# Half of a weight matrix loaded during attention, a weight test handed from VectorE to GpSimd, and one wait of ScalarE put on another instruction

## The chip, the cores and the metric

The kernel runs on one core of a Trainium2 chip. It is one program on one core: TensorE (PE), VectorE (DVE), ScalarE (ACT) and GpSimd (POOL) each work through their own instructions in order, and DMAs are issued in order on queues that belong to an engine: the queue of SyncE (SP), of ScalarE and of GpSimd. The metric is the device time of one execution in microseconds (us), as the median of several runs. Lower is better.

## The reference

`x` is 4 batches of 1024 tokens with 256 channels, float32. There are 16 heads of 16 channels, and the hidden width of the feed-forward part is 1024. The weights of the feed-forward part are ternary (-1, 0 or 1) with a scale per output.

```
x = x + layernorm(attention(layernorm(x)))       # q, k, v, p: alpha * sign(W), softmax over 1024 keys
x = x + layernorm(ffn(layernorm(x)))

def ffn(x):
    h = silu(x @ w1.T * s1) * (x @ w2.T * s2)    # 256 -> 1024
    h = gelu(h @ h1.T * sh1)                     # 1024 -> 1024
    h = gelu(h @ h2.T * sh2)                     # 1024 -> 1024
    return h @ w3.T * s3                         # 1024 -> 256
```

## The kernel before, in words

Products run in TensorE's reduced-precision float format (`F32R`), with every activation split into a high and a low piece, so that two products give nearly full precision. The weights are taken as they are, in one piece. That is right only when their low bits are zero, as they are for ternary weights. So the kernel looks at every weight of the feed-forward part during attention: it collects their low bits in the tile `bits`, reduces them at the end to a flag (`any_bits`, `decide`), and branches on the flag before the feed-forward part to `mlp("", False, ...)` or to a slower form. With these inputs the fast form runs.

**Attention** is a loop over steps `s`, written out in the order of the program. A step handles 128 keys for a block of 512 queries and four heads; 8 steps make a block (`STEPS`), 16 steps a unit `u` of four heads (2 blocks), 64 steps a batch, and there are 256 steps. Each step has two halves. In a half step TensorE does six products of the second pass (`second_pass`, L690), four of the first pass (`first_pass`, L642) for a step that lies ten steps ahead, and the product of the weights with `v` for the step before (`attend`, L707). VectorE takes the row maximum of the first pass (`first_max`, L652) and ScalarE the exponential of the second pass (`second_exp`, L695), both out of PSUM. The exponentials go to tiles `e` from a pool of five buffers, two exponentials for each tile.

Everything else is a job in the dictionary `jobs`, which `place` puts behind a half step `(s, slot)`; `run_jobs` issues the jobs of a half step at its end, and so they stand on each engine's queue at that place. The jobs that matter here, for unit `u` that starts to be used by the first pass at `s = 16u - 10`:

- `group_jobs` (for even `u`): the q and k projections of the next two units, in four `part`s at `16u - 24, -22, -20, -18`, slot 1. Each is a product, a ScalarE copy out of PSUM (L500), and on GpSimd a cast and a subtraction (L506, L507) that write the high and low pieces to the tiles q0, q1, k0, k1. Each of the four tiles is 128 x 1024 in float32 and has one buffer.
- `spread(u)` at `16u - 16`, slot 0: 24 DMAs on SyncE's queue (L530) that copy rows of these pieces to the layout of the products, `qs` and `ks` with two buffers each. The first-pass products of a new unit wait for the first 12 in its first half step and for the last 12 in its second.
- `batch_jobs`: norms, transposes and `v` of the next batch; `project_jobs`: the output projection of the finished batch (z times `az_bc` plus `bz_bc` on GpSimd at L574 and L575), its moments, and `finish_tile` on GpSimd (L589, L592).
- `turn_y`, `divide`, `return_y`: the result of a block is transposed on VectorE (L727), divided on GpSimd (L733), transposed back on VectorE (L748) and sent by four DMAs on SyncE's queue (L751).
- `weight_jobs`: loads of `w1`, the first half of `h1` (`h1a_sb`) and `w2` on GpSimd's queue (L821); then 44 `gather` jobs, one for each 128 x 512 tile of the weights, that put its bits into `bits` (L835). The first 12 and the last 4 take tiles that stay; the 28 between take tiles that are only looked at (second half of `h1`, `h2`, `w3`), loaded into `wraw` with two buffers. `take(i)` gathers tile i and then issues the load of tile i + 2 on SyncE's queue (L840), which waits until the gather has read the buffer.

`tc.add_manual_dep(a, b)` makes instruction a wait for instruction b. A tile of a pool that comes round again makes its first writer wait for what last wrote and read that buffer; an instruction carries one wait, and what it has to wait for besides goes into a waiting instruction put ahead of it.

**The feed-forward part** (`mlp`) loads the second half of `h1` (`h1b_sb`, 2 MB in 2 DMAs), then `h2` (4 MB) and `w3` on GpSimd's queue (L1009) once GpSimd has finished its last work of attention. It then runs 8 blocks of 512 tokens: `gated` (w1 and w2), `hidden` with `h1`, `hidden` with `h2` (all products at L1063) and `down` (L1177).

Of the kernel before, what the change touches and what calls it, by code (L numbers as in the profile page):

```python
# [30 lines left out]
F32 = mybir.dt.float32  # L31
F32R = mybir.dt.float32r
I32 = mybir.dt.int32
AF = mybir.ActivationFunctionType
ALU = mybir.AluOpType
AX = mybir.AxisListType
# [3 lines left out]
P = 128  # L40
# [5 lines left out]
def sandwich_kernel(  # L46
# [23 lines left out]
    nc = tc.nc  # L70
# [35 lines left out]
    w1_sb = const.tile([P, KC, F], F32R, tag="w1", name="w1_sb")  # L106
    w2_sb = const.tile([P, KC, F], F32R, tag="w2", name="w2_sb")
    h1a_sb = const.tile([P, NF // 2, F], F32R, tag="h1a", name="h1a_sb")


    xnT_sb = const.tile([P, KC, T], F32R, tag="xnT", name="xnT_sb")
# [114 lines left out]
    def attention(signs):  # L226


        with ExitStack() as actx:
# [83 lines left out]
            nc.gpsimd.memset(negmax, 0.0)  # L313

            a2 = actx.enter_context(tc.tile_pool(name="a2", bufs=2))
            a3 = actx.enter_context(tc.tile_pool(name="a3", bufs=5))
            av = actx.enter_context(tc.tile_pool(name="av", bufs=1))

            def binarize(w, sgn, dst):
# [159 lines left out]
            def group_jobs(grp):  # L479

                b, c = divmod(grp, KC)

                def part(is_q, j, engine=nc.gpsimd):
                    tag = "q" if is_q else "k"
                    if j == 0:
                        pieces_of[grp, is_q] = [
                            ac.tile([P, T], F32R, tag=f"{tag}{i}", name=f"{tag}{i}_{grp}")
                            for i in range(2)
                        ]
                    t = bank(grp > 0)  # L490
# [14 lines left out]
                    hi, lo = (t[:, bass.ts(j, 512)] for t in pieces_of[grp, is_q])  # L505
                    engine.tensor_copy(hi, full)  # L506
                    engine.tensor_sub(lo, full, hi.bitcast(F32))  # L507

                if grp == 0:
                    return part  # L510
                return [lambda i=i, j=j: part(i, j) for i in (True, False) for j in range(NQ)]
# [179 lines left out]
                    [nmT_by[blk]] if n == 2 else [],  # L691
                )

            def second_exp(s, g, t):
                got([t], "ACT", nc.scalar.activation(  # L695
                    e_of[s][g // 2][:, g % 2, :], through[:, t, :], AF.Exp
                ))

            def attend(s, part):

# [51 lines left out]


            jobs = {}
            beside_pe = []

            def place(at, job, on_pe=False):
                jobs.setdefault(at, []).append(job)
                if on_pe:
                    beside_pe.append(at)  # L760

            first = -STEPS - LEAD
            for b in range(1, B):
                norms, turns, values = batch_jobs(b)
                at = b * NG * NQ * STEPS + first
                for i, job in enumerate(norms):
                    place((at - 32 + i // 2, i % 2), job)
                for i, job in enumerate(turns):
                    place((at - 18 + i // 2, i % 2), job, True)

                for i, job in enumerate(values):
                    place((at - first - STEPS + 3 + 2 * i, 0), job, True)
            for u in range(1, B * NG):
                at = u * NQ * STEPS + first
                if u % 2 == 0:
                    for job, when in zip(group_jobs(u // 2), (-14, -12, -10, -8)):
                        place((at + when, 1), job, True)
                place((at - 6, 0), lambda u=u: spread(u))
            for b in range(B):
                for half in range(2 if b < B - 1 else 1):  # L780
                    at = (((b + 1) * NG - 1) * NQ + half + 1) * STEPS + (6, 10)[half]
                    pieces, projects, measures, finishes = project_jobs(b, half)
                    for i, job in enumerate(pieces):
                        place((at - 2, i), job)
                    for i, job in enumerate(projects):
                        place((at + i, 1), job, True)
# [21 lines left out]


            raw_of = {}  # L810
            bits = ac.tile([P, 512], I32, tag="bits", name="bits")
            nc.gpsimd.memset(bits, 0)

            def weight_jobs():
# [17 lines left out]
                        ]  # L832

                def gather(w):
                    nc.vector.tensor_tensor(bits, bits, w.bitcast(I32), ALU.bitwise_or)  # L835

                def load(i):
                    if i < len(pass_by):
# [10 lines left out]

                def any_bits():  # L850

                    nc.vector.tensor_scalar(bits, bits, 0xFFF, None, ALU.bitwise_and)
                    nc.vector.tensor_reduce(some, bits, AX.X, ALU.max)
                    nc.vector.tensor_scalar(some, some, 0.0, None, ALU.is_gt)

# [18 lines left out]

            free = (B * NG - 2) * NQ * STEPS + first - 6
            place((free, 0), last)
            at = 44
            for job in gathers + last_gathers:
                if job is last_gathers[0]:
                    at = max(at, free + 6)  # L880
                at, slot = min((k for k in beside_pe if at + 3 <= k[0] <= at + 5), default=(at + 4, 1))
                place((at, slot), job)

            def run_jobs(s, slot):
                for job in jobs.pop((s, slot), ()):
# [21 lines left out]
            for s in range(first, total + 2):  # L907
# [4 lines left out]
                for half in range(2):  # L912


                    second_of, first_of = [], []
                    if second:
                        e_of[s].append(a3.tile([P, 2, 512], F32, tag="e", name=f"e_{s}_{half}"))
                    two, pair = take(2 * second, 2 * (a < total))
                    if second:
                        second_of = list(zip((2 * half, 2 * half + 1), two))  # L920
                    if a < total:

                        first_of = [
                            (2 * (1 - half) + t - min(pair), t, begin) for begin, t in enumerate(pair)
                        ]
                    for n in range(3):
                        for g, t in second_of[:1]:
                            second_pass(s, g, t, n)
                        for g, t, begin in first_of:
                            if 0 <= n - begin < 2:  # L930
                                first_pass(a, g, t, n - begin)
                        for g, t in second_of[1:]:
                            second_pass(s, g, t, n)
                    for g, t in second_of[:1]:
                        second_exp(s, g, t)
                    if a < total:
                        first_max(a, pair, 1 - half)
                    if 0 <= s - 1 < total:
                        attend(s - 1, half)
                    if s > 0 and (s % STEPS, half) == (0, 1):  # L940
                        fetch_y(s // STEPS - 1)
                    for g, t in second_of[1:]:
                        second_exp(s, g, t)
# [11 lines left out]
    def mlp(tag, low_too, wp):  # L955
        with ExitStack() as fctx:

            def pool(name, bufs, **space):
# [11 lines left out]

            blocks = B * T // 512
            per_batch = T // 512
            h1b_sb = fw.tile(
                [P, NF // 2, F], F32R, tag="h1b", name="h1b_sb" + tag
            )
            h2_sb = fw.tile([P, NF, F], F32R, tag="h2", name="h2_sb" + tag)
            w3_sb = fw.tile([P, NF, C], F32R, tag="w3", name="w3_sb" + tag)

            w1_w, w2_w, h1_w, h2_w, w3_w = (
                (w1_sb,), (w2_sb,), (h1a_sb, h1b_sb), (h2_sb,), (w3_sb,)  # L980
            )

            def rows(w, k):
# [16 lines left out]
                )  # L1000
                return raw[:, :n, :]

            for dst, wT, parts in (
                (h1b_sb, h1T[F // 2 : F, :], 2), (h2_sb, h2T, 4), (w3_sb, w3T, 1)
            ):
                n = dst.shape[1] // parts
                for i in range(parts):
                    ks = bass.ts(i, n)
# [320 lines left out]
```

## Time and profile before

| What | Value |
|---|---|
| median of 3 runs (lowest to highest) | 1643.37 us (1639.27 to 1645.26) |
| profiled execution, its own time | 1643.64 us |
| profiled execution, span of the instructions | 1641.8 us |
| busy share PE / DVE / ACT / POOL | 96% / 66% / 51% / 21% |
| attention, from its first to its last product | about 45 to 968 us |
| 44 gathers on DVE (L835) | 32.7 us busy |
| mean granted TensorE clock | 0.981 |

All times of the profile are of one execution. A group of instructions has a line, an engine and an operation; behind the bar stand its busy time and the mean of one in ns, and then the idle time of the engine just before it with what ended that idle time. The TensorE clock is the share of full speed that was granted.

### The profile page before, as it was taken

What the parts mean: (1) busy time and instruction counts of PE and PEld (TensorE: products, weight loads), DVE (VectorE), ACT (ScalarE), POOL (GpSimd) and SP (SyncE); (2) the same over time, 40 slices, a digit from 0 to 9 for tenths busy, and PEclk for the clock granted to TensorE, in tenths of its full rate; (3) what the DMA queues carried; (4) which work ended last, traced back from release to release, by engine and by line L of the source; (5) the groups of instructions that cost most, each with busy time, mean ns of one, the idle gap of its engine ahead of it and who ended that gap; (6) DMA issues with size and microseconds to landing.
All of it is one profiled execution on the core that took longest, in us unless ns stands there. A gap on an engine that the chain in (4) does not pass through costs nothing.

```text
span 1641.8 us, 31481 instructions
## 1 busy us (share of the span) xinstructions
PE 1574.0 (96%) x12964; PEld 1010.1 (62%) x12964; DVE 1079.7 (66%) x1497; ACT 844.2 (51%) x1481; POOL 347.7 (21%) x484
## 2 busy tenths in 40 slices
PE   4699999999999999999999998999999999999997
PEld 3344444544445444445544457888888888888886
DVE  4578878889887889787789633563636363535453
ACT  2067777776777676777776771132323232323231
POOL 1011320454011343104511042120202020202011
PEclk9689999999999999999999999999999999999999
DMA  1502242202331232132122005000000000000000
GB/s 56 105 2 46 63 90 47 43 19 71 69 64 42 49 69 52 38 66 43 24 53 47 5 7 179 1 13 1 13 1 13 1 14 0 14 0 14 1 14 16
DMA packets 35673, 60.10 MB, mean 37 GB/s; under 512 B 10176, under 2 KB 21696, under 8 KB 35520
## 3 DMA queue, kind: packets, MB, share of 16 engines
q1 hardware_dynamic: 29568, 44.35, 12.7%
q0 software_dynamic: 3760, 11.54, 2.2%
q10 hardware_dynamic: 2192, 2.10, 0.6%
q8 instruction: 104, 1.70, 0.4%
q14 instruction: 49, 0.40, 0.1%
HBM read 24.40 MB, written 4.19 MB: 17 GB/s over the span
## 4 chain that ended last, share of the span: by engine, by line
PE 83%; DVE 9%; DMA 2%; ACT 1%; POOL 1%; issue 1%; SPq 1%; ACTq 0%; DVEq 0%; POOLq 0%
PE g L1063 28%; PE through L690 18%; PE y L707 14%; PE p L1063 7%; PE through L642 6%; DVE nm L652 6%; PE fzp L1177 4%; PE through L493 2%; DMA qs<-q 1%; PE through L670 1%; PE through L560 1%; SPq L530 1%; PE through L451 1%; DMA ks<-k 1%; DVE bits L835 1%
## 5 line engine op out<-in xcount | busy, mean ns | idle before, releaser
L652 DVE TENSOR_REDUCE nm<-through 128x2 f32<-128x1024 f32 x512 | 619.6, 1217 | 144.6 <-PE through L690 107.2
L695 ACT ACTIVATE e<-through 128x512 f32<-128x512 f32 x1024 | 557.3, 596 | 216.4 <-PE through L690 178.7
L642 PE MATMUL through<-ks,qs 32*128 32x512 f32 x2048 | 473.8, 452 | 15.6 <-DMA ks<-k 10.9
L690 PE MATMUL through<-qs,ks 32*128 32x512 f32 x2048 | 397.8, 448 | 13.0 <-DVE nm L652 12.5
L707 PE MATMUL y<-e,v 128*32 128x256 f32 x4096 | 337.5, 393 | 0.0
L690 PEld LDWEIGHTS through<-qs,ks 32*128 32x128 f32 x2048 | 203.0, 184 | 213.1 <-issue 134.1
L642 PEld LDWEIGHTS through<-ks,qs 32*128 32x128 f32 x2048 | 240.3, 187 | 28.4 <-issue 12.1
L1063 PE MATMUL g<-g,h_sb 128*128 128x512 f32 x1024 | 235.8, 390 | 0.0
L690 PE MATMUL through<-nmT,ones_r 32*128 32x512 f32 x1024 | 219.9, 394 | 0.0
L1063 PEld LDWEIGHTS g<-g,h_sb 128*128 128x128 f32 x1024 | 191.7, 188 | 39.6
L707 PEld LDWEIGHTS y<-e,v 128*32 128x32 f32 x4096 | 83.8, 108 | 193.3 <-issue 174.4
L1106 ACT ACTIVATE g2f<-g,sh_sb 128x512 f32<-128x512 f32 x64 | 44.1, 688 | 200.5 <-PE g L1063 173.6
L1106 ACT ACTIVATE g1f<-g,sh_sb 128x512 f32<-128x512 f32 x64 | 44.0, 689 | 177.8 <-PE g L1063 174.9
L1063 PE MATMUL g<-h,h1b_sb 128*128 128x512 f32 x512 | 127.8, 392 | 4.6 <-DMA h1b_sb<-in_dram 4.6
L1063 PE MATMUL g<-h,h1a_sb 128*128 128x512 f32 x512 | 128.1, 393 | 0.0
L1033 DVE CAST g<-g2f 128x512 fp32r<-128x512 f32 x64 | 27.8, 434 | 142.0 <-ACT g2f L1106 142.0
L1063 PE MATMUL p<-xnT_sb,w_sb 128*128 128x512 f32 x512 | 118.0, 390 | 1.2 <-DVE hf L1139 1.2
L690 PEld LDWEIGHTS through<-nmT,ones_r 32*128 32x128 f32 x1024 | 108.9, 185 | 6.1
L1063 PEld LDWEIGHTS g<-h,h1b_sb 128*128 128x128 f32 x512 | 96.9, 190 | 25.1 <-issue 5.0
L1063 PEld LDWEIGHTS g<-h,h1a_sb 128*128 128x128 f32 x512 | 97.2, 190 | 20.5
L1063 PEld LDWEIGHTS p<-xnT_sb,w_sb 128*128 128x128 f32 x512 | 95.5, 188 | 21.6 <-DVE hf L1139 1.7
L146 POOL TENSOR_SCALAR ve_fz<-mvp_fz 128x4 f32<-128x4 f32 (+1 forms) x8 | 1.9, 233 | 470.8 <-DVE mvp_fz L158 470.8
(173 smaller groups left out, 1438.9 us busy)
## 6 DMA issues: line engine op xcount, KB each, us to landing
qs<-q SPq DMA_DIRECT2D x248, 64.0 KB, 2.4
ks<-k SPq DMA_DIRECT2D x124, 64.0 KB, 2.4
wraw<-in_dram SPq DMA_DIRECT2D x28, 256.0 KB, 2.7
h_sb<-in_dram POOLq DMA_DIRECT2D x4, 1024.0 KB, 11.5
yT<-yt SPq DMA_DIRECT2D x112, 32.0 KB, 1.9
out_dram<-x_sb SPq DMA_DIRECT2D x7, 512.0 KB, 2.8
x_sb<-in_dram SPq DMA_DIRECT2D x3, 1024.0 KB, 6.0
w_sb<-in_dram POOLq DMA_DIRECT2D x3, 1024.0 KB, 8.7
```

The lines of the kernel that those rows point to most:

```text
L451: put(t, nc.tensor.matmul(through[:, t, bass.ts(i, C)], xnT[j][:, k, bass.ts(2 * m + i, P)], w_in["v"][:, k, :], start=(k == 0 and j == 0) ...
L493: put(t, nc.tensor.matmul(through[:, t, :], w_in[tag][:, k, bass.ts(c, P)], xnT[i][:, k, bass.ts(j, 512)], start=(k == 0 and i == 0), stop ...
L530: queue.dma_start(dst[to, :].bitcast(F32), src[rows, :].bitcast(F32))
L642: put(t, nc.tensor.matmul(through[:, t, :], q_of[u][n][rows, bass.ts(qt, P)], k_of[u][rows, bass.ts(j, 512)], start=(n == 0), stop=(n == 1),))
L652: got(banks, "DVE", nc.vector.tensor_reduce(nm_of[blk][:, n4, j, 2 * pair : 2 * pair + 2], through[:, min(banks) : max(banks) + 1, :], AX. ...
L690: t, nc.tensor.matmul(through[:, t, :], lhs, rhs, start=(n == 0), stop=(n == 2)),
L695: got([t], "ACT", nc.scalar.activation(e_of[s][g // 2][:, g % 2, :], through[:, t, :], AF.Exp))
L707: nc.tensor.matmul(y_of[blk][32 * g : 32 * g + 32, cols], v_sb[n // 2][:, n % 2, :, :].rearrange("p h d -> p (h d)")[:, bass.ds((4 * g4 + ...
L1033: nc.vector.tensor_copy(hi, full)
L1063: nc.tensor.matmul(out[c], wk, src[j][:, k, :], start=(k == 0 and i == 0 and j == 0), stop=(k == n_k - 1 and i == len(ws) - 1 and j == 1),)
L1106: nc.scalar.activation(g, ps, AF.Gelu, scale=scale[:, c : c + 1])
L1177: nc.tensor.matmul(out_ps[i][:, :C], g2[j][:, k, bass.ts(i, P)], wk, start=(k == 0 and n == 0 and j == 0), stop=(k == NF - 1 and n == len( ...
```

## The change

- The four tiles q0, q1, k0, k1 become the four tiles `h1b0` to `h1b3` of the constant pool, each 128 x 1 x 1024. When the last spread has read them, four loads of 0.5 MB on GpSimd's queue at steps 226 to 229 fill them with the second half of `h1`. `mlp` loads only `h2` and `w3`.
- A `gather` is two GpSimd operations: a copy that turns the low 16 bits of each weight (every second half word) into floats, and an addition to `bits`, now float32. The mask with 0xFFF in `any_bits` goes; the rest of `any_bits` stays on VectorE.
- The gathers get other places. Before, each went 3 to 5 steps behind the last, beside a job with products where there was one. Now the first 40 go at steps 47, 51, ..., slot 1 (every step that is 3 or 7 modulo 8); the load of the first two `wraw` tiles takes one of these places. The last four gathers, `any_bits` and `decide` go at steps 214 to 219.
- The second exponential of each `e` tile gets a manual dependence on the second exponential four tiles before it, which is the one whose buffer the next tile takes. The wait of ScalarE for itself then stands on the second exponential of a tile, no longer on the first.

The order of the products, of ScalarE's instructions and of the DMAs other than those of `wraw` and `h1b` stays as it was; `decide`'s product comes earlier.

```diff
+    h1b_sb = [
+        const.tile([P, 1, F], F32R, tag=f"h1b{i}", name=f"h1b{i}_sb") for i in range(NF // 2)
+    ]
...
                         pieces_of[grp, is_q] = [
-                            ac.tile([P, T], F32R, tag=f"{tag}{i}", name=f"{tag}{i}_{grp}")
-                            for i in range(2)
+                            t[:, 0, :] for t in (h1b_sb[:2] if is_q else h1b_sb[2:])
                         ]
...
-            def second_exp(s, g, t):
-                got([t], "ACT", nc.scalar.activation(
+            def second_exp(s, g, t, last):
+                exp = got([t], "ACT", nc.scalar.activation(
                     e_of[s][g // 2][:, g % 2, :], through[:, t, :], AF.Exp
                 ))
+                if last:
+                    last_exps.append(exp)
+                    if len(last_exps) > E_TILES - 1:
+                        tc.add_manual_dep(
+                            exp, last_exps[-E_TILES].name, SYNC, reason="the next tile"
+                        )
...
-            bits = ac.tile([P, 512], I32, tag="bits", name="bits")
+            bits = ac.tile([P, 512], F32, tag="bits", name="bits")
...
                 def gather(w):
-                    nc.vector.tensor_tensor(bits, bits, w.bitcast(I32), ALU.bitwise_or)
+                    low = w.bitcast(U16).rearrange("p (c half) -> p c half", half=2)[:, :, 0]
+                    half = ac.tile([P, 512], F32, tag="half", name="half")
+                    nc.gpsimd.tensor_copy(half, low)
+                    nc.gpsimd.tensor_add(bits, bits, half)
...
                 def any_bits():
-                    nc.vector.tensor_scalar(bits, bits, 0xFFF, None, ALU.bitwise_and)
                     nc.vector.tensor_reduce(some, bits, AX.X, ALU.max)
...
+            for i, to in enumerate(h1b_sb):
+                place(
+                    (free + NQ * STEPS + 2 + i, 0), lambda to=to, i=i: nc.gpsimd.dma_start(
+                        to[:, 0, :], h1T.rearrange("(k p) o -> p k o", p=P)[:, NF // 2 + i, :]
+                    ),
+                )
             at = 44
             for job in gathers + last_gathers:
                 if job is last_gathers[0]:
                     at = max(at, free + 6)
-                at, slot = min((k for k in beside_pe if at + 3 <= k[0] <= at + 5), default=(at + 4, 1))
-                place((at, slot), job)
+                while at % STEPS not in (3, 7) and job not in last_gathers:
+                    at += 1
+                place((at, 1), job)
+                at += 1
...
-            h1b_sb = fw.tile(
-                [P, NF // 2, F], F32R, tag="h1b", name="h1b_sb" + tag
-            )
...
-            for dst, wT, parts in (
-                (h1b_sb, h1T[F // 2 : F, :], 2), (h2_sb, h2T, 4), (w3_sb, w3T, 1)
-            ):
+            for dst, wT, parts in ((h2_sb, h2T, 4), (w3_sb, w3T, 1)):
```

More of the change, by code (lines that the diff above doesn't have):

```diff
@@ L33 @@
 I32 = mybir.dt.int32
+U16 = mybir.dt.uint16
 AF = mybir.ActivationFunctionType
@@ L315, in attention @@
             a2 = actx.enter_context(tc.tile_pool(name="a2", bufs=2))
-            a3 = actx.enter_context(tc.tile_pool(name="a3", bufs=5))
+            E_TILES = 5
+            a3 = actx.enter_context(tc.tile_pool(name="a3", bufs=E_TILES))
             av = actx.enter_context(tc.tile_pool(name="av", bufs=1))
@@ L692, in second_pass @@
                 )
-            def second_exp(s, g, t):
-                got([t], "ACT", nc.scalar.activation(
+            last_exps = []
+            def second_exp(s, g, t, last):
+                exp = got([t], "ACT", nc.scalar.activation(
                     e_of[s][g // 2][:, g % 2, :], through[:, t, :], AF.Exp
                 ))
+                if last:
[4 more added lines that the diff above has]
+                        )
             def attend(s, part):
@@ L754, in attention, with place @@
             jobs = {}
-            beside_pe = []
-            def place(at, job, on_pe=False):
+            def place(at, job):
                 jobs.setdefault(at, []).append(job)
-                if on_pe:
-                    beside_pe.append(at)
             first = -STEPS - LEAD
@@ L768, in attention @@
                 for i, job in enumerate(turns):
-                    place((at - 18 + i // 2, i % 2), job, True)
+                    place((at - 18 + i // 2, i % 2), job)
                 for i, job in enumerate(values):
-                    place((at - first - STEPS + 3 + 2 * i, 0), job, True)
+                    place((at - first - STEPS + 3 + 2 * i, 0), job)
             for u in range(1, B * NG):
@@ L776, in attention @@
                     for job, when in zip(group_jobs(u // 2), (-14, -12, -10, -8)):
-                        place((at + when, 1), job, True)
+                        place((at + when, 1), job)
                 place((at - 6, 0), lambda u=u: spread(u))
@@ L785, in attention @@
                     for i, job in enumerate(projects):
-                        place((at + i, 1), job, True)
+                        place((at + i, 1), job)
                     for i, job in enumerate(measures):
@@ L934, in attention @@
                     for g, t in second_of[:1]:
-                        second_exp(s, g, t)
+                        second_exp(s, g, t, False)
                     if a < total:
@@ L942, in attention @@
                     for g, t in second_of[1:]:
-                        second_exp(s, g, t)
+                        second_exp(s, g, t, True)
                     run_jobs(s, half)
@@ L979, in mlp @@
             w1_w, w2_w, h1_w, h2_w, w3_w = (
-                (w1_sb,), (w2_sb,), (h1a_sb, h1b_sb), (h2_sb,), (w3_sb,)
+                (w1_sb,), (w2_sb,), [h1a_sb[:, i : i + 1, :] for i in range(NF // 2)] + h1b_sb,
+                (h2_sb,), (w3_sb,),
             )
```

## The prediction

> **What bounds the kernel now.** I read the page first, for the engine that carries the end.
>
> ```profile
> PE 83%; DVE 9%; DMA 2%; ACT 1%; POOL 1%; issue 1%; SPq 1%; ACTq 0%; DVEq 0%; POOLq 0%
> L652 DVE TENSOR_REDUCE nm<-through 128x2 f32<-128x1024 f32 x512 | 619.6, 1217 | 144.6 <-PE through L690 107.2
> L1063 PE MATMUL g<-h,h1b_sb 128*128 128x512 f32 x512 | 127.8, 392 | 4.6 <-DMA h1b_sb<-in_dram 4.6
> ```
>
> The chain is TensorE's for 83%. In the timeline a plain half step of attention lasts 1.467 us, all of it products, and VectorE needs 1.217 us of it for the row maximum, which leaves it 0.25 us. So work taken from VectorE pays only where its 0.25 us run out. The third row gives TensorE's one named wait behind attention. Next the timeline of TensorE there, and the windows (columns: length, then busy time and count of PE, PEld, DVE, ACT, POOL, then granted clock, DMA share, GB/s):
>
> ```profile
> 984.51 1.97 PE L1063 MATMUL g<-h,h1a_sb 128*128 128x512 f32 x8
> 991.06 2.04 PE L1063 MATMUL g<-h,h1b_sb 128*128 128x512 f32 x4 [4.57 <-DMA h1b_sb<-in_dram]
> ...
> 986.50:991.00 4.50, 0.00 (x0) 0.00 (x0) 0.40 (x1) 1.18 (x2) 4.42 (x6) 0.92 0.87 293
> 991.00:997.00 6.00, 5.94 (x14) 4.72 (x15) 0.00 (x0) 0.00 (x0) 0.00 (x0) 0.50 1.13 417
> ```
>
> TensorE stands 4.57 us for `h1b_sb`, then works at half clock. Last, a place where a gather hurts: the chain of waits about 560 us, GpSimd's timeline there, and windows there and one batch later, at the same steps without a gather.
>
> ```profile
> 560.65 1.77 DVE bits L835
> 560.10 1.78 POOL L507 TENSOR_TENSOR q<-full_True,q 128x512 fp32r<-128x512 f32 x1
> 560.20:563.60 3.40, 1.61 (x22) 0.69 (x18) 3.40 (x4) 1.81 (x4) 1.68 (x1) 1.00 0.05 8
> 563.60:567.00 3.40, 3.38 (x26) 1.76 (x28) 2.95 (x4) 1.08 (x2) 0.62 (x1) 0.50 0.20 69
> 560.20:570.40 10.20, 8.40 (x62) 4.10 (x59) 8.20 (x9) 3.98 (x8) 2.30 (x2) 0.67 0.08 26
> 787.50:797.70 10.20, 9.89 (x111) 5.25 (x103) 8.32 (x10) 7.13 (x14) 5.22 (x6) 1.00 0.05 12
> ```
>
> The gather, 0.68 us elsewhere, takes 1.77 us beside L507; TensorE loses half a window and then runs one at 0.50.
>
> **The change part by part.** The sum is made against the profiled execution, 1643.64 us (span 1641.8), which stands 0.3 us above the median of 1643.37.
>
> *h1's half.* The wait of 4.57 us goes. So does the half clock behind it: 6.83 us (990.26 to 997.08) at 0.50 hold 3.41 us of full-speed work. Together −8.0. What is late next would be `h2`: its four loads start at 985.6 in both kernels at best (GpSimd's last L592), land in a median of 11.5 us, the four in about 10 more at the 417 GB/s of the window, and are first needed near 1013: nothing. The four new loads are issued at steps 226 to 229, after the last spread (861.7 to 877.1), on GpSimd's queue, where the combine of step 229 has a step to spare; nothing else is queued to a deadline. Cost 0.
>
> *Gathers off VectorE.* 44 take 32.7 us, but most lie in half steps where TensorE has extra products (about 1.14 us for four of L493 or eight of L560) and cover them. I took each half step's length over 1.467 us and compared it with the same half step of a batch without the gather: 336 us, 1.85 against 0.19, gain 1.66; 560.65 with the two half steps after it, 4.64 against 0.24, gain 4.40 (half clock included); 628, 0.6; 374 and 601, 0.22 each; 383 and 610, 0.3 together; 848, 0.25; `any_bits` at 892 to 901, 2.4, of which about 0.6 stay at its new place. Sum −9.45, taken as −9.5. The rest was hidden beside products and brings nothing.
>
> *The same work on GpSimd.* The copy has no row. Nearest is L506, a cast of the same 128x512: 0.61 to 0.65 us. From above, L589 and L422 take 1.22 to 1.26 us for 256 elements, so 2.45 for 512. I take 0.65, since it is the same shape and also a conversion; the addition is L507, 1.28. So 1.9 us each, 44 make 84 us, on an engine that is busy 348 of 1642. Rule: the Trainium skill, "GPSIMD Engine Reference", section 3.1, gives about 1.8 cycles per element for the best one-input loop (512 elements measured at 769 ns) and 2.6 for two inputs, 1.11 us by its 1.2 GHz; against the rows, 0.12 to 0.16 us more on the copy and 0.17 less on the addition. The sum below would change by at most 0.4 us; I keep the rows. VectorE's reduces are unharmed: L652 takes 1.22 us with GpSimd busy or idle. GpSimd's divide (L733) can come up to 0.3 us later, three times with an effect: +0.5.
>
> *A new wait on SyncE's queue.* In `take(i)` the load of `wraw` must wait until the gather's copy has read its buffer. That copy is now behind everything GpSimd has queued. A load stands at step 16u−17, slot 1, directly ahead of the 24 DMAs of spread u. Now:
>
> ```profile
> 588.20 0.33 SPq L840 DMA_DIRECT2D wraw<-in_dram  x1
> 588.72 1.29 POOL L507 TENSOR_TENSOR k<-full_False,k 128x512 fp32r<-128x512 f32 x1
> 589.29 1.15 SPq L530 DMA_DIRECT2D qs<-q  x2
> 592.75 0.73 POOL L592 TENSOR_TENSOR x_sb<-x_sb,z 128x256 f32<-128x256 f32 x1
> 604.65 0.59 SPq L530 DMA_DIRECT2D ks<-k  x1
> 609.81 0.18 PEld L642 LDWEIGHTS through<-ks,qs 32*128 32x128 f32 x1
> ```
>
> Unit 10: the spread starts at 589.29, its last DMA goes at 604.65 and lands 2.4 us later, 2.8 us before its user at 609.81. In the changed kernel the copy stands after L592: 593.48 + 0.65 = 594.1, then the load's 0.4 us; the spread starts about 594.6, 5.2 us late, so its tail is 2.4 us late. Unit 9: z's addition (L575) ends 531.85 and the copy 532.5; the spread goes from 526.01 to 533.0, 7.0 late against a margin of 5.9 counted to the first product in need: 1.1 us. Unit 13: 753.54 to 760.5, 1.2 us. Units 8 and 12 move by 1.6 us inside margins of 2.9 and 3.0, unit 11 has 7.0, and 14 and 15 have no load ahead. Behind this queue nothing but `yT` waits; it has slack. Sum +4.7. Bounds: −0 (if the wait is satisfied sooner, the spreads are on time) and, with the copy at 2.45 us, units 8, 9, 10, 12 and 13 later by 1.8 each, about +13.
>
> *Half clock after the late spread.* By the Trainium skill, "TensorE: Matmul & The Clock Gate", section "What's actually happening", the clock falls to half after an idle window of about 3.4 us, on a free-running grid of 3413 ns. Read so, a stall of 2.4 us costs no clock, and the sum is 3.4 lower. The row above speaks against it: in the window from 560.20, 1.61 of 3.40 us were busy, and the next was granted 0.50. Windows 56% busy and more kept theirs. So an idle of over about 1.6 us within one window decides; 2.4 us does that in roughly two of three positions on the grid, 1.1 and 1.2 us do not alone. I take one fall: +3.4 (bounds 0 and 10, for none and three).
>
> *ScalarE's wait.* Its own wait stood on a tile's first exponential and now stands on the second, for an exponential four tiles back, long done. A satisfied wait between two of ScalarE's instructions shows no gap in the timeline (starts 0.477 to 0.488 us apart with or without), and TensorE sets the pace: 0, bounds −2 and +1. The order of the exponentials is unchanged.
>
> Sum: 1643.6 − 8.0 − 9.5 + 0.5 + 4.7 + 3.4 = 1634.7.
>
> **The rivals.** *No fall of the clock* (the skill's rule, or luck with the grid): 1631.3. For: phase is chance. *Spreads not late*: if GpSimd runs ahead of the places I read, or the copy waits less, both last terms go, 1626.6. Against: the instruction that the load waits for stands behind L592 in GpSimd's order, and L592's chain starts only after VectorE's moments. *More falls*: a copy of 1.2 us makes units 9 and 13 1.7 us late and 10 3 us; two or three falls, 1638 to 1642. *Slower*: the strided read of half words runs at the pace of L589, 2.45 us a copy. The five spreads then cost 4.7 + about 8, two more falls 6.8, and the divides and k pieces behind 3.7-us gathers some 4 us: about 1654. It breaks even where the copy passes 1.9 us. For: no row of 16-bit reads; against: L506 of the same shape. *The change does not do what it says*: the early loads of `h1b` wait for something later than the last spread, or `h2` takes the place of the stall; the 8.0 is lost, 1642.
>
> **How the numbers follow.** What a measurement of this kernel tells from no change is 0.5%, 8.2 us: faster means under 1635.2, slower over 1651.6. Chances: late spreads with one fall (1634.7, give or take 3) 0.36, half of it faster; without a fall (1631.3) 0.23, of which 0.19 faster; spreads on time (1626.6) 0.18, faster; more falls 0.13, same; no gain from `h1b` 0.03, same; slow copy 0.07, slower. That makes faster 0.55, same 0.38, slower 0.07. The forecast is the first case's, 1634.5 beside the median (0.3 under the execution). From 1625 to 1641.5 the range takes in all but the slow copy, the lost gain and the tails of two cases.
>
> **What would show it.** In the changed profile: no wait for `h1b`, and the clock at 1.00 from 984 to 997 (right), or a wait for `h_sb` there (wrong). TENSOR_COPY on GpSimd at 0.65 us (right; at over 1.9 us the forecast fails). On SyncE's queue the spread of unit 10 starting some 5 us behind where `q` and `k` were ready, and TensorE's idle before L642 for `ks<-k` up from 10.9 us by about 5, most of it in units 9, 10 and 13, and a window at 0.50 behind unit 10; if that idle stays near 10.9, the last two terms fall away. The half clock behind 560 gone. If L652's mean rises over 1.22 us, I am wrong on contention.

## The result and the profile after

The changed kernel takes 1632.91 us in the median of 6 runs (1632.26 to 1636.19), against 1644.00 (1639.27 to 1645.26) for the kernel before in the runs beside it. The ratio is 0.9939 with an interval of 0.9925 to 0.9954, so between 7.6 and 12.3 us were gained. The profiled execution took 1632.26 us, with a span of 1630.5. The forecast was 1634.5, in a range of 1625.0 to 1641.5.

These are the lines of the page and of the chain of waits' first row that answer to those shown of before. Most line numbers have moved: L652 is now L657, L690 is L695, L707 is L722 and L1063 is L1083.

```profile
PE 84%; DVE 6%; SPq 2%; POOL 2%; ACT 2%; DMA 1%; issue 1%; ACTq 0%; DVEq 0%
L657 DVE TENSOR_REDUCE nm<-through 128x2 f32<-128x1024 f32 x512 | 620.8, 1218 | 166.4 <-PE through L695 133.4
L1083 PE MATMUL g<-h,h1b_sb 128*128 128x512 f32 x512 | 126.4, 389 | 0.0
```

The share of VectorE in the chain fell from 9% to 6%, and SyncE's queue and GpSimd, at 1% each before, stand at 2%: some of what VectorE gave up, the queue and GpSimd took. The row maximum still takes 1.218 us, with 80 us more of work on GpSimd. The products with `h1b_sb` wait for nothing. TensorE's timeline at the start of the feed-forward part, and windows there (columns as in the prediction: length, then busy time and count of PE, PEld, DVE, ACT, POOL, then granted clock, DMA share, GB/s):

```profile
981.00 1.98 PE L1083 MATMUL g<-h,h1a_sb 128*128 128x512 f32 x8
982.81 1.07 PE L1083 MATMUL g<-h,h1b_sb 128*128 128x512 f32 x4
983.72 1.98 PE L1083 MATMUL g<-h,h1a_sb 128*128 128x512 f32 x8
...
982.00:988.00 6.00, 6.00 (x28) 4.98 (x27) 1.29 (x3) 2.12 (x3) 3.91 (x5) 1.00 0.74 240
988.00:994.00 6.00, 6.00 (x28) 4.96 (x27) 2.85 (x6) 2.07 (x3) 0.00 (x0) 1.00 1.12 420
```

The wait of 4.57 us is gone, the clock is at 1.00, and the loads of `h2` (420 GB/s in the second window) come in time for their products at 1010.0.

Now the place of the late spreads. The first block is the timeline of SyncE's queue and GpSimd for unit 10, the second its product of TensorE, the third holds windows behind unit 10 and unit 13.

```profile
582.42 1.23 POOL L594 TENSOR_SCALAR z<-z,mvp_z,rsp_z 128x256 f32<-128x256 f32 x1
583.74 0.73 POOL L597 TENSOR_TENSOR x_sb<-x_sb,z 128x256 f32<-128x256 f32 x1
584.42 0.61 POOL L849 CAST half<-wraw 128x512 f32<-128x512 uint16 x1
585.05 0.33 SPq L855 DMA_DIRECT2D wraw<-in_dram  x1
585.44 1.15 SPq L535 DMA_DIRECT2D qs<-h1b_sb  x2
...
603.50 0.75 PE L647 MATMUL through<-ks,qs 32*128 32x512 f32 x1 [1.96 <-DMA ks<-h1b_sb]
...
600.10:603.51 3.41, 1.45 (x19) 0.50 (x16) 1.94 (x5) 1.09 (x2) 0.58 (x3) 1.00 0.50 94
603.51:606.93 3.42, 3.42 (x21) 1.63 (x25) 1.74 (x3) 1.21 (x3) 0.00 (x0) 0.50 0.36 99
606.93:610.34 3.41, 3.41 (x28) 1.66 (x28) 1.74 (x3) 1.55 (x3) 0.00 (x0) 0.50 0.01 5
770.77:774.18 3.41, 2.25 (x26) 0.81 (x21) 1.57 (x2) 1.59 (x4) 3.18 (x7) 1.00 0.36 72
774.18:777.59 3.41, 3.41 (x26) 1.76 (x22) 1.31 (x2) 1.60 (x4) 1.93 (x3) 0.50 0.53 163
```

The copy follows GpSimd's L597, the load follows the copy at once, and the spread follows the load. The product of unit 10 then waits 1.96 us for `ks` (its source is called `h1b_sb` now, since the pieces of q and k lie in the tiles `h1b0` to `h1b3`), and two windows of 3.41 us pass at half clock. One more passes at half clock behind unit 13. The prediction's sign for this, TensorE's idle time ahead of the first pass for `ks`, was to go up from 10.9 us by about 5. It went up by 4.0, before and after:

```profile
L642 PE MATMUL through<-ks,qs 32*128 32x512 f32 x2048 | 473.8, 452 | 15.6 <-DMA ks<-k 10.9
...
L647 PE MATMUL through<-ks,qs 32*128 32x512 f32 x2048 | 458.1, 452 | 19.3 <-DMA ks<-h1b_sb 14.9
```

Attention has the other side of the ledger. I laid the starts of its 512 half steps (the first weight load of `attend`) of both traces side by side and noted each half step whose length changed:

| Where (end of the half step, us in the trace before) | Change of length, us |
|---|---|
| 340, 438, 631, 665: a gather went from there | −1.65, −0.60, −0.54, −0.60 |
| 565 to 572: a gather and a half clock went | −2.35, −0.86, −1.18 |
| 884 and 903: `any_bits` and `decide` went | −0.35, −1.43 |
| 851: `any_bits` and `decide` came | +1.12 |
| 550, unit 9 late | +1.08 |
| 611 to 615, unit 10 late and half clock | +2.94, +1.15, +0.91 |
| 720, unit 12 late | +0.48 |
| 778 to 780, unit 13 late and half clock | +1.64, +1.22 |
| the 489 half steps that changed by under 0.25 each | −3.81 in sum |

With 0.27 at attention's start and five other changes of under 0.8 (−0.9 in sum), attention ends 3.50 us sooner, and the feed-forward part gives the other 7.8 of the 11.3 us between the two spans.

### The profile page after: what moved, and what is told of

Read it like the earlier page. It is cut to its first block, busy times and chain, and to the rows that moved or that the text cites. A ratio compares the mean times of both kernels' runs of the same rounds, so it can differ in the third digit from the quotient of the medians.

```text
span 1630.5 us, 31482 instructions
## 1 busy us (share of the span) xinstructions
PE 1568.3 (96%) x12964; PEld 1007.4 (62%) x12964; DVE 1053.6 (65%) x1452; ACT 846.9 (52%) x1481; POOL 428.1 (26%) x574
## 4 chain that ended last, share of the span: by engine, by line
PE 84%; DVE 6%; SPq 2%; POOL 2%; ACT 2%; DMA 1%; issue 1%; ACTq 0%; DVEq 0%
PE g L1083 28%; PE through L695 17%; PE y L722 15%; PE p L1083 7%; PE through L647 7%; DVE nm L657 4%; PE fzp L1197 4%; SPq L535 2%; PE through L498 2%; PE through L675 1%; DMA ks<-h1b_sb 1%; PE through L565 1%; PE through L457 1%; PE through L440 1%; ACT e L704 1%
## 5 line engine op out<-in xcount | busy, mean ns | idle before, releaser
L657 DVE TENSOR_REDUCE nm<-through 128x2 f32<-128x1024 f32 x512 | 620.8, 1218 | 166.4 <-PE through L695 133.4
L647 PE MATMUL through<-ks,qs 32*128 32x512 f32 x2048 | 458.1, 452 | 19.3 <-DMA ks<-h1b_sb 14.9
L695 PE MATMUL through<-qs,ks 32*128 32x512 f32 x2048 | 396.4, 448 | 7.7 <-DVE nm L657 6.7
L722 PE MATMUL y<-e,v 128*32 128x256 f32 x4096 | 337.5, 393 | 0.0
L695 PEld LDWEIGHTS through<-qs,ks 32*128 32x128 f32 x2048 | 186.9, 184 | 206.2 <-issue 138.8
L647 PEld LDWEIGHTS through<-ks,qs 32*128 32x128 f32 x2048 | 225.1, 187 | 32.0 <-issue 15.5
L1083 PE MATMUL g<-g,h_sb 128*128 128x512 f32 x1024 | 235.7, 390 | 0.0
L695 PE MATMUL through<-nmT,ones_r 32*128 32x512 f32 x1024 | 218.4, 395 | 0.0
L1083 PEld LDWEIGHTS g<-g,h_sb 128*128 128x128 f32 x1024 | 191.7, 188 | 39.5
L722 PEld LDWEIGHTS y<-e,v 128*32 128x32 f32 x4096 | 83.9, 108 | 193.5 <-issue 174.5
L1083 PE MATMUL g<-h,h1a_sb 128*128 128x512 f32 x512 | 126.4, 389 | 0.0
L1083 PE MATMUL g<-h,h1b_sb 128*128 128x512 f32 x512 | 126.4, 389 | 0.0
L1083 PE MATMUL p<-xnT_sb,w_sb 128*128 128x512 f32 x512 | 118.0, 390 | 1.2 <-DVE hf L1159 1.2
L695 PEld LDWEIGHTS through<-nmT,ones_r 32*128 32x128 f32 x1024 | 107.6, 185 | 5.6
L1083 PEld LDWEIGHTS p<-xnT_sb,w_sb 128*128 128x128 f32 x512 | 95.5, 188 | 21.5 <-DVE hf L1159 1.7
L1083 PEld LDWEIGHTS g<-h,h1a_sb 128*128 128x128 f32 x512 | 96.1, 188 | 20.0
L1083 PEld LDWEIGHTS g<-h,h1b_sb 128*128 128x128 f32 x512 | 96.1, 188 | 19.9
```

What stands on the lines that cost most here:

```text
L647: put(t, nc.tensor.matmul(through[:, t, :], q_of[u][n][rows, bass.ts(qt, P)], k_of[u][rows, bass.ts(j, 512)], start=(n == 0), stop=(n == 1),))
L657: got(banks, "DVE", nc.vector.tensor_reduce(nm_of[blk][:, n4, j, 2 * pair : 2 * pair + 2], through[:, min(banks) : max(banks) + 1, :], AX. ...
L695: t, nc.tensor.matmul(through[:, t, :], lhs, rhs, start=(n == 0), stop=(n == 2)),
L722: nc.tensor.matmul(y_of[blk][32 * g : 32 * g + 32, cols], v_sb[n // 2][:, n % 2, :, :].rearrange("p h d -> p (h d)")[:, bass.ds((4 * g4 + ...
L1083: nc.tensor.matmul(out[c], wk, src[j][:, k, :], start=(k == 0 and i == 0 and j == 0), stop=(k == n_k - 1 and i == len(ws) - 1 and j == 1),)
```

## The experiments

Differences are against the kernel before, run beside each kernel. Its median was 1644.76 us beside the first four kernels below, 1642.38 us beside the third buffer, the old places and the later test, and 1644.48 us beside the others. Where two kernels with different runs of before are compared by their medians, up to 2.4 us of the difference can come from that.

**h1's half alone.** The four tiles, their loads at steps 226 to 229, and nothing else:

```diff
-                            ac.tile([P, T], F32R, tag=f"{tag}{i}", name=f"{tag}{i}_{grp}")
-                            for i in range(2)
+                            t[:, 0, :] for t in (h1b_sb[:2] if is_q else h1b_sb[2:])
...
-                (h1b_sb, h1T[F // 2 : F, :], 2), (h2_sb, h2T, 4), (w3_sb, w3T, 1)
+            for dst, wT, parts in ((h2_sb, h2T, 4), (w3_sb, w3T, 1)):
```

> Before, with only the second half of h1 loaded during attention. My theory (the wait of 4.57 us and the half clock behind it both go, nothing takes their place): 8.0 us less than before, about 1636. Rival (the loads of h2 or their own late start take the place of the wait): less than 3 us gained, 1641 to 1644.

Measured: 1635.22 us (1633.03 to 1639.71), ratio 0.995 (0.9934 to 0.9967), so 8.2 us gained, between 5.4 and 10.9. This part does what was counted.

**The gathers alone.** GpSimd's copy and addition at the new places; q's and k's tiles, `h1b_sb` and ScalarE's wait as before:

```diff
-                    nc.vector.tensor_tensor(bits, bits, w.bitcast(I32), ALU.bitwise_or)
+                    low = w.bitcast(U16).rearrange("p (c half) -> p c half", half=2)[:, :, 0]
+                    half = ac.tile([P, 512], F32, tag="half", name="half")
+                    nc.gpsimd.tensor_copy(half, low)
+                    nc.gpsimd.tensor_add(bits, bits, half)
...
-                at, slot = min((k for k in beside_pe if at + 3 <= k[0] <= at + 5), default=(at + 4, 1))
-                place((at, slot), job)
+                while at % STEPS not in (3, 7) and job not in last_gathers:
+                    at += 1
+                place((at, 1), job)
+                at += 1
```

> Before, with only the gathers on GpSimd at their new places (h1's half and ScalarE's wait as before). My theory: all that attention gained in the changed kernel's trace, 3.5 us net (gathers' gain of 12 to 14 less about 10 of late spreads and clock), is made here: about 1640.5, with the spreads of units 9, 10 and 13 late as in the changed kernel. Rival (part of that gain is ScalarE's wait): 1643 to 1646.

Measured: 1643.12 us (1639.32 to 1649.03), ratio 0.9995 (0.998 to 1.0009). That is 0.8 us gained, between 3.3 gained and 1.5 lost. By the same side-by-side comparison units 9, 10 and 13 are late here too, and the gains at the old places are the same. So the largest part of the edit brings nothing that can be measured: what it saves at the old places it loses on SyncE's queue. Part of what attention gained in the changed kernel must then come from elsewhere.

**ScalarE's wait alone.**

```diff
+                if last:
+                    last_exps.append(exp)
+                    if len(last_exps) > E_TILES - 1:
+                        tc.add_manual_dep(
+                            exp, last_exps[-E_TILES].name, SYNC, reason="the next tile"
+                        )
```

> Before, with only the dependence that moves ScalarE's own wait to the second exponential. My theory (TensorE sets the pace, a satisfied wait costs nothing): within 1 us of before, 1643 to 1645. Rival (the 4 to 5 us that attention gained beyond my sum come from here): 1639 to 1640.

Measured: 1641.18 us (1638.31 to 1644.39), ratio 0.9981 (0.9971 to 0.9992): 3.1 us gained, between 1.3 and 4.8. My expectation of nothing fell. The rows of ScalarE's exponential, before and in this kernel, with all the releasers of its idle time:

```profile
L695 ACT ACTIVATE e<-through 128x512 f32<-128x512 f32 x1024 | 557.3, 596 | 216.4 <-PE through L690 178.7 <-PE through L642 35.5
L700 ACT ACTIVATE e<-through 128x512 f32<-128x512 f32 x1024 | 557.1, 596 | 210.4 <-PE through L691 198.7 <-PE through L643 10.8
```

The time that ScalarE waits for the first pass (L642, here L643) fell from 35.5 to 10.8 us, while the wait for the second pass grew. One half step of each trace shows what moves; the first three lines are of before, the last three of this kernel:

```profile
448.63 0.16 PEld L707 LDWEIGHTS y<-e,v 128*32 128x32 f32 x8 [0.37 <-issue]
448.79 1.09 ACT L695 ACTIVATE e<-through 128x512 f32<-128x512 f32 x2
449.44 0.49 PE L642 MATMUL through<-ks,qs 32*128 32x512 f32 x1
...
449.53 0.16 PEld L718 LDWEIGHTS y<-e,v 128*32 128x32 f32 x8 [0.37 <-issue]
449.63 1.09 ACT L700 ACTIVATE e<-through 128x512 f32<-128x512 f32 x2
450.28 0.50 PE L643 MATMUL through<-ks,qs 32*128 32x512 f32 x1
```

The first exponential starts 0.16 us after the first weight load of `attend` before and 0.10 us here, and a product of the first pass 0.81 and 0.75 us. Over plain half steps the exponential starts at 0.156 and 0.100 us (medians of 177 and 188 half steps). The weight load of that first-pass product waits, in both traces, for the semaphore that the exponential sets, and goes a median of 42 and 43 ns behind it (361 and 326 loads); it moves up by 55 ns. The median half step shrinks from 1.473 to 1.470 us. All nine kernels of this study with the moved wait have 1.469 or 1.470 us there, and the four without it 1.473 or 1.474. The 501 half steps that changed by under 0.25 us sum to −2.2 us here, against +0.33 with h1's half alone. So it is a small gain in every half step.

**The load behind the spread.** In the changed kernel, `take(i)` no longer issues its load; a job of its own does, one step later where the gather stands directly ahead of a spread:

```diff
                     gather(raw_of.pop(i))
-                    load(i + 2)
...
+                if 13 <= n < len(gathers):
+                    later = at % 16 == 15
+                    place((at + later, 1), lambda i=n - 11: load(i))
```

> The changed kernel, with the wraw load of every gather at step 16u-17 put one step later, behind the 24 DMAs of the spread. My theory (that load holds SyncE's queue until GpSimd's copy is done, and so makes units 9, 10, 12 and 13 late): no wait for ks above 0.5 us in those units, no half clock at 603 and 774, 9 to 10 us less than the changed kernel, about 1623.5. Rival (the spreads are late because GpSimd makes the pieces late, or because the DMAs themselves are slower): as the changed kernel, 1633.

Measured: 1623.79 us (1623.51 to 1625.14), ratio 0.9873 (0.9856 to 0.9891). The interval does not touch that of the changed kernel. No spread of units 8 to 13 is late, and the granted clock is 1.00 from 93.7 to 1616 us. The 9 us that the medians lie apart were lost on that queue.

**One place only.** The same with `later = at == 143`, so that the load moves only ahead of unit 10.

> The changed kernel, with the load behind the spread at one place only, step 143 (unit 10). My theory: 2.3 us of wait and the 3.4 us of half clock behind it go, units 9, 12 and 13 stay late: 5.7 us less than the changed kernel, about 1627. Rival (the half clock has another cause than this wait): 2.3 us less, 1630.5.

Measured: 1627.03 us (1626.21 to 1629.96), ratio 0.9895 (0.9872 to 0.9917), 5.9 us below the changed kernel by the medians. Unit 9 is still 1.3 us late and unit 13 1.3, and in this trace no window behind them fell to half clock. One place held most of the loss.

**A third buffer.** Here the loads stay ahead of the spreads, but find a buffer that was read long ago:

```diff
-raw_of[i] = a2.tile([P, 512], F32, tag="wraw", name=f"wraw_{i}")
+raw_of[i] = a2.tile([P, 512], F32, tag="wraw", name=f"wraw_{i}", bufs=3)
```

> The changed kernel with three buffers for wraw instead of two; the loads stay ahead of the spreads on SyncE's queue, but wait for a gather that was done 4 steps earlier. My theory (the wait for the copy makes the spreads late, not the load's place in the queue or its bytes): spreads on time, 1623 to 1625. Rival (the load itself ahead of the spread, its 256 KB and its issue, is what costs): 1629 to 1633.

Measured: 1623.35 us (1621.94 to 1624.05), ratio 0.9877 (0.9858 to 0.9896). So it is the wait, not the load or its place. The waits of SyncE's queue show it; the first row is of before, the second of the changed kernel, the third of this one (engine and line, what was waited for, us in total, times, longest).

```profile
SPq L840 <- DVE bits L835: 116.6, 15, 12.8
...
SPq L855 <- POOL half L849: 119.5, 16, 21.6
...
SPq L855 <- POOL half L849: 8.9, 4, 6.1
```

The total hardly differs between the first two; what changed is which of the waits stand ahead of something with a deadline.

**The copy twice.** In the changed kernel, each gather's `nc.gpsimd.tensor_copy(half, low)` is issued twice.

> The changed kernel with GpSimd's copy done twice in each gather (0.61 us more each, 27 us more on GpSimd). My theory (only the late spreads feel it): units 9, 10, 12 and 13 0.6 us later each, 2.4 us in all, and none to two more halves of the clock of 1.7 to 3.4 us: 1635 to 1640. Rival (GpSimd's time is hidden, spreads have another cause): 1633. Rival (GpSimd's other work is late too): over 1642.

Measured: 1639.11 us (1635.35 to 1642.86), ratio 0.9968 (0.9955 to 0.9981), 6.2 us above the changed kernel. Unit 9 is 1.5 us late, unit 10 2.7, unit 12 0.6 and unit 13 3.4, by the landing of the last DMA against the first product in need. In the changed kernel these are 1.2, 2.3, 0.5 and 1.7. Behind unit 13 three windows are at half clock where one was, behind unit 10 one where two were. Away from these units the half steps show a longer copy at two places only: 0.66 us more where VectorE waits for GpSimd's divide (1.24 us at 825.62 us of this trace, 0.59 at 821.15 in the changed kernel's), and 0.33 at 324 us.

**No gathers.** Before, with the or-operation only for the first tile; 43 gathers are left out.

> Before, with 43 of the 44 gathers left out (only the first tile's bits are collected; the loads of wraw stay). What the gathers cost before in all: my theory 8 to 9 us (1.7 at 336 us, 4.4 at 560 with its half clock, 0.6 at 437, 630 and 665 each, some 0.2 at eight more places), so 1635 to 1637; the any_bits at the end stays. Rival (all hidden beside TensorE): 1643 to 1645. Rival (also the part beside extra products costs): 1630 or less.

Measured: 1632.90 us (1631.75 to 1634.67), ratio 0.9922 (0.9901 to 0.9943): 12.8 us, between 9.4 and 16.3. It is somewhat more than the 8 to 9 expected. The losses by name are those of the table above (−1.68, −0.61, −4.40, −0.61, −0.60). The half clock behind 560 us, 2.7 of the 4.4, belongs to one trace: with h1's half alone it went too, though the gather stayed, and in another trace it falls elsewhere, as the next experiment shows. With the gathers on GpSimd alone the time was 1643.12 us, so the hand-over as made took away almost none of this cost: what went from VectorE came back on SyncE's queue.

**VectorE at the new places, and at the old ones.** The first is the changed kernel with the gather of before (an or on VectorE, and the mask in `any_bits`). The second is before with h1's half and ScalarE's wait.

```diff
-                    nc.gpsimd.tensor_copy(half, low)
-                    nc.gpsimd.tensor_add(bits, bits, half)
+                    nc.vector.tensor_tensor(bits, bits, w.bitcast(I32), ALU.bitwise_or)
```

> The changed kernel, but each gather is VectorE's one or-operation again (and any_bits masks), at the changed kernel's places. My theory (the engine makes the gathers' gain, and GpSimd's copy makes the late spreads): spreads on time again, 10 us gained; but at places without extra products each gather of 0.68 us has 0.25 us of slack and costs TensorE some 0.4, 40 of them 16 us: 1636 to 1640. Rival (the new places make the gain, on either engine): 1623 to 1626.

> Before with h1's half loaded during attention and ScalarE's wait moved, the gathers on VectorE at their old places. Against the same with VectorE's gathers at the new places (1628.6) it gives the worth of the places, and against the loads behind the spreads (1623.8) that of the engine. My theory now (the places carry about half): 1633, from 1644.5 less 8.2 and 3. Rival (the places carry nothing, VectorE's gathers cost the same anywhere): 1628.6.

Measured: 1628.59 us (1627.40 to 1629.78), ratio 0.9901 (0.9879 to 0.9922), at the new places; 1634.81 us (1632.09 to 1640.22), ratio 0.9955 (0.9933 to 0.9977), at the old ones. So with the gathers on VectorE the new places (the test's too) bring 6.2 us by the medians and 8.9 by the ratios.

What GpSimd brings over VectorE is not isolated by these runs. The kernel with VectorE's gathers is 4.3 us faster than the changed one (1632.91) and 4.8 slower than the one with the loads behind the spreads (1623.79). But its own loads still stand ahead of the spreads, and in its trace units 12 and 14 are 0.8 and 1.2 us late. Against the trace with the loads behind the spreads their half steps are 0.84 and 1.05 us longer, and the test's, which masks again, 0.68. Attention is 3.3 us longer in all, so under 1 us is left for the engine itself in these two traces. This is rough, for their executions lie 2.3 us apart and the medians 4.8. VectorE's gathers at the new places with the loads behind the spreads, or with a third buffer, were not run.

The expected cost of 16 us for uncovered gathers was wrong: the half steps show no loss over 0.25 us at most of the gathers in plain half steps. What hurt at the old places were single collisions with GpSimd's L511 (L507 before). The tile's rows at the old and at the new places, then windows at the old places:

```profile
L849 DVE TENSOR_TENSOR bits<-bits,wraw x28: 649/681/1774, 412.1 to 749.2; 128x512 int32<-128x512 int32 x28
...
L847 DVE TENSOR_TENSOR bits<-bits,wraw x28: 660/681/1152, 425.0 to 804.8; 128x512 int32<-128x512 int32 x28
...
337.40:344.20 6.80, 6.80 (x40) 3.40 (x36) 4.25 (x6) 2.50 (x5) 0.62 (x1) 0.50 0.03 7
627.50:634.30 6.80, 6.80 (x54) 2.35 (x46) 3.82 (x4) 2.97 (x6) 1.85 (x2) 0.50 0.16 51
```

At the old places the longest takes 1.774 us, at the new ones 1.152. At the old places the clock fell to half at 337 and 627 us in this trace, where it fell at 563 us in the one of before. At the new places with VectorE it stayed at 1.00 from 92.5 to 1618 us.

**The test later.** As with the loads behind the spread, and `any_bits` and `decide` at steps 226 and 228.

> As the changed kernel with all loads of steps 16u-17 behind the spread, and any_bits and decide moved from steps 218 and 219 to 226 and 228. At 218 any_bits stood right behind a transpose and the traces showed 1.1 us lost there. My theory: 0.5 to 1 us less than with the loads moved alone, 1623. Rival (any_bits costs the same wherever no product covers it): 1623.8.

Measured: 1623.98 us (1622.58 to 1625.99), ratio 0.9885 (0.9867 to 0.9902). The half steps show 0.61 and 0.26 us lost at the new place, where 1.14 were lost at the earlier one, but the time does not tell it from the kernel with the loads moved alone. This stays open; if it gains, it is under 1 us.

The best kernels of the study are the changed one with a third buffer, or with the loads behind the spreads: 1623.35 and 1623.79 us, some 9 us below the change as made.

## Why the prediction was right, and where it was off

*h1's half.* The step stood at −8.0; alone it measured −8.2. Nothing was late in its place, and `h2` came in time.

*Gathers off VectorE.* The step stood at −9.5. The side-by-side half steps give −7.8 for the named places, some −2 for small ones, and −0.7 for the test: about −10.4, so the size is near. 2.7 of the −7.8 are the half clock behind 560 us, which goes without any change to the gathers too; that it was in the trace of before was chance. The test was mis-sized, −1.8 where −0.7 came. At step 218 it stands right behind a transpose of VectorE, but in the last experiment it does too, and 0.6 and 0.3 were lost there, so the cause stays open. The reason given for the whole step was in the main wrong. I put the gain down to the engine; with VectorE kept, the new places alone bring 6.2 us or more, and the traces show under 1 us for the engine. I had the evidence in hand: both 1.77-us gathers of before stood beside GpSimd's L507, which is a matter of place.

*GpSimd's divide.* +0.5 was taken. At one place, 821 us in the changed kernel's trace, VectorE waits 0.59 us for it, and the half step is 0.31 us longer.

*The copy.* 0.65 us was taken from the cast; the profile of the changed kernel has 0.61 for the copy and 1.28 for the addition. The slower rival, with 2.45 us, is out.

```profile
L849 POOL CAST half<-wraw x28: 604/611/620, 418.4 to 813.7; 128x512 f32<-128x512 uint16 x28
L850 POOL TENSOR_TENSOR bits<-bits,half x44: 1269/1279/1289, 246.3 to 844.1; 128x512 f32<-128x512 f32 x44
```

*The new wait on SyncE's queue.* Forecast: units 9, 10 and 13 late by 1.1, 2.4 and 1.2 us. In the trace: 1.2, 2.3 and 1.7, and unit 12, which was counted as safe, by 0.5. The sum of 4.7 should have been 5.7. TensorE's idle time for `ks` rose by 4.0, so not all of the lateness was lost. Both ways of taking the wait away, and doubling the copy, moved the time as this step says.

*Half clock behind it.* One fall, +3.4, was taken; the trace has three half-clock windows, 5.1 us: two behind unit 10, which make the 3.4, and one behind unit 13, which was counted as none. (The prediction says that one window was at 0.50 behind 560 us. There were two, as the 0.67 over three windows in its own lines shows.) The row of the trace was right and the rule of the Trainium skill ("TensorE: Matmul & The Clock Gate", "What's actually happening"), read so that a stall shorter than an idle window costs nothing, was not: 1.45 of 3.41 us were busy and the next two windows were at 0.50. But my own bound, that windows 56% busy and more keep their clock, did not hold either: ahead of the fall behind unit 13, 2.25 of 3.41 us were busy, 66%, and one window was at half. Together the late spreads and the clock stood at +8.1; the half steps of units 9, 10, 12 and 13 grew by 9.4, and moving the loads took 9.1 away.

*ScalarE's wait.* Forecast 0 with bounds of −2 and +1; alone it measured −3.1 (−4.8 to −1.3). This is the step that failed. A satisfied wait shows no gap between two of ScalarE's instructions, but ahead of the first exponential it added 56 ns, and the argument that TensorE sets the pace missed that one of TensorE's own first-pass weight loads waits for that exponential.

The three parts alone gained 8.2, 0.8 and 3.1 us, 12.1 in sum, and the change 11.1 (7.6 to 12.3). For the largest part the forecast, −9.5 + 0.5 + 4.7 + 3.4 = −0.9, met the −0.8. What brought the total 1.6 us below the forecast is in the main ScalarE's term, put at 0. Within the largest part the errors cancel: about 0.9 us more from the gathers and 0.2 less lost at the divide, against 1.3 more for the spreads with their clock. The gathers' gain and the clock's loss both hang on the windows in which a trace has its stalls, so that agreement is in part luck. What is left, about 1 us, lies in changes at the start and near 215 us, which other traces show in other sizes and for which I have no cause.

## What to carry to other kernels

When an operation is handed to an idle engine, look at what was waiting for the old one: here a DMA's buffer, and behind that DMA 24 others with a deadline. One more buffer brought some 9 us to the changed kernel, where the hand-over alone had brought 0.8.

Try the new places without the new engine before putting a gain down to the engine. And a wait of some 2 us of TensorE is to be counted with the half clock that may follow it.

## What the runs showed of the hardware that was not expected

A window of 3.41 us in which TensorE was 66% busy was followed by one window at half clock, one at 43% by two. But in the same trace windows 64% and 56% busy (from 968.7 and 1033.6 us, 2.17 and 1.91 of 3.40) kept the clock at 1.00, so the busy share of the records alone does not decide. In which window the clock falls changes from trace to trace, and the old places of the gathers left several such stalls. This fits the ranges: all times of before lie between 1639.3 and 1648.3 us, those of the kernel with a third buffer, whose clock stays at 1.00 from 91.7 to 1614 us in its trace, between 1621.9 and 1624.1. Over the 46 runs of before beside the experiments, the span falls as the mean granted clock rises: from 1646.4 us at 0.975 to 1637.8 at 0.984, with a correlation of −0.83. So most of the spread goes with the clock; which of the two leads is not shown by that, since a stall makes both.

A copy that reads every second 16-bit word of 128x512 and writes floats took GpSimd 0.61 us, as much as the plain cast of the same shape. And 56 ns of ScalarE, ahead of work that looked hidden, were worth about 3 ns of TensorE in the median of some 500 half steps.
